# Rotary sums of q and k: accumulating DMAs in place of GpSimd additions

## The chip, the cores and the metric

The kernel runs on one core of a Trainium2 chip. A core has five engines that follow instruction streams of their own: TensorE (PE: matmuls and transposes), VectorE (DVE), ScalarE (ACT), GpSimd (POOL) and SyncE (SP, which issues DMAs), and 16 DMA engines that move data. The metric is the device time of one execution in microseconds (us), lower is better. The kernel before takes 3546.09 us, the median of three runs (3543.17 to 3550.35).

## The reference

The input x has 8 sequences of 512 tokens with 128 features, in float32. It is normalised, and two branches are added to it: an attention with relative positions (16 heads of 8), and a stack of six layers, each a local attention (16 heads of 64, windows of 32) and a gated feed-forward part. The change lies in the local attention, where q and k are normalised per head and rotated:

```python
def attn_layer(x, Wqkv, qs, ksc, Wo):
    qkv = x @ Wqkv
    q, k, v = jnp.split(qkv, 3, -1)
    ...
    q = l2norm(q) * qs
    k = l2norm(k) * ksc
    ...
    q = q * cos * scale + rotate_half(q) * sin * scale
    k = k * cos * inv + rotate_half(k) * sin * inv
    out = local_attention(q, k, v)
    ...
    return out @ Wo
```

## The kernel before

There are two stages. The relative attention (`rel_attention`) takes up about the first 470 us. The layers (`steps_of_layers`) follow: 6 layers x 8 sequences x 4 blocks of 128 tokens are 192 tiles, numbered by `tiles`. Weights are reloaded for each layer. x stays transposed in SBUF (`xt`).

The tiles run in a software pipeline. The loop at L1113 takes a tile n, and a word from `ORDERS` (line 48) sets the order of steps within it: `p0` to `p3` project tile n+2, `r` normalises it, `q0 q1 k0 k1` transpose q and k of tile n+1 on TensorE (`turn`, L818), `s0 s1` are the scores and the softmax of tile n, `v0` to `v3` its values, `a0 a1` apply the softmax of tile n-1, `+` adds tile n-2 into `xt`, and `f` is one step of a feed-forward. There are four such words, one for each tile of a sequence. TensorE keeps the order in which the program is written (`manual_schedule`). The order on the other engines is chosen when the program is built, by a timeline that the scheduler keeps, so a change of one step can move others.

For a tile, `project(n, c)` runs four times: c = 0, 1 for the two halves of q, c = 2, 3 for those of k. TensorE makes a half (128 tokens x 512) in PSUM out of three matmuls (L637 to L639). VectorE multiplies it twice, by the cosine table into `q` (L762) and by the sine table into `rot` (L763), with the halves of each head exchanged, and ScalarE squares it into `sq` (L764). When the second half is there, GpSimd adds `rot` to `q`, 128 x 1024 (L767). For q GpSimd also adds the two halves of `sq` (L769), and VectorE sums them per head into `ss` (L770); for k VectorE sums both halves itself (L772). `normalise` (step `r`) works out the inverse roots `rn` on VectorE (L782, and L70 to L81 in `rsqrt`), and GpSimd scales first q and then k by them (L786). The buffers are rings: 4 of `q`, 3 of `rot`, 2 of `sq`, so a buffer of `rot` is written again three sums later.

Beside this, GpSimd scales the softmax (`pr`, L888, which waits for the sums `sm` inverted at L887), and makes some low parts (L626) and diagonal matrices (`dg`, L985) for the feed-forward. Values are copied out of PSUM by ScalarE (`v`, L904, 3 buffers) and laid out anew by 16 DMAs of 64 KB per tile from SyncE's queue (`vw`, L906); TensorE reads them at L924. ScalarE's exponentials (L871) wait for the row maxima `mx` of VectorE (L858).

Of the kernel before, what the change touches and what calls it, by code (L numbers as in the profile page):

```python
# [16 lines left out]
ALU = mybir.AluOpType  # L17
# [572 lines left out]
def steps_of_layers(ctx, tc, i, ident, ident_b, xt, out, spare):  # L590
    nc = tc.nc
# [41 lines left out]
    def product(ps, lhs, rhs):  # L633


        (ah, al), (bh, bl) = lhs, rhs
        nc.tensor.matmul(ps, lhsT=ah, rhs=bh, start=True, stop=False)  # L637
        nc.tensor.matmul(ps, lhsT=ah, rhs=bl, start=False, stop=False)  # L638
        nc.tensor.matmul(ps, lhsT=al, rhs=bh, start=False, stop=True)  # L639
# [96 lines left out]
    def halves(xs, t):  # L736
        return [x[:, t * P : (t + 1) * P] for x in xs]

    def project(n, c):

        part, a = divmod(c, 2)
        l, b, t = tiles[n]
        if c == 0:
            ready[n] = {"ss": pq.tile([P, 2, H], F32, name="ss")}
        if a == 0:
            ready[n][part] = [
                pq.tile([P, H, 2, D // 2], F32, name="q", bufs=4),
                pq.tile([P, H, 2, D // 2], F32, name="rot", bufs=3),
                pq.tile([P, 2, H, D // 2], F32, name="sq"),
            ]  # L750
        q, v, sq = ready[n][part]
        xs, w, ss = streams[l, b], projections[l, part], ready[n]["ss"]
        cos, sin = (
            tables[l, t][:, 2 * part + m, :].rearrange("p (a d) -> p a d", a=2) for m in range(2)
        )

        def wide(x):
            return x.unsqueeze(1).to_broadcast([P, H, D // 2])

        ps = ps_qk.tile([P, H, D // 2], F32, name="qk_ps")  # L760
        product(ps.rearrange("p h d -> p (h d)"), halves(xs, t), w[a])
        nc.vector.tensor_mul(q[:, :, a], ps, wide(cos[:, a, :]))  # L762
        nc.vector.tensor_mul(v[:, :, 1 - a], ps, wide(sin[:, 1 - a, :]))  # L763
        nc.scalar.activation(sq[:, a], ps, AF.Square)  # L764
        if a == 0:
            return
        nc.gpsimd.tensor_add(q, q, v)  # L767
        if str(part) in VAR["C"]:
            nc.gpsimd.tensor_add(sq[:, 0], sq[:, 0], sq[:, 1])  # L769
            nc.vector.tensor_reduce(ss[:, part, :], sq[:, 0], AX.X, ALU.add)  # L770
        else:
            nc.vector.tensor_reduce(  # L772
                ss[:, part, :], sq.rearrange("p a h d -> p h a d"), AX.XY, ALU.add
            )
        ready[n][part] = q.rearrange("p h a d -> p h (a d)")
# [311 lines left out]
    for n in range(2):  # L1087
        for c in range(4):
            project(n, c)
            if c == 3:  # L1090
                normalise(n)
            yield
# [19 lines left out]
    with tc.manual_schedule(engines={nc.tensor.engine}):  # L1112
        for n in range(-1, len(tiles) + 2):  # L1113
# [10 lines left out]
            for step in ORDERS[n % NT].split():  # L1124
                kind, k = step[0], int(step[1:] or 0)
                if kind == "p" and more:
                    project(n + 2, k)
                    l, b, t = tiles[n + 2]
                    if k == 3 and b == B - 1 and l + 1 < DEPTH:
# [123 lines left out]
```

## Time and profile before

| | us |
|---|---|
| median of three runs | 3546.09 |
| profiled execution, its own time | 3550.94 |
| its span, first to last instruction | 3549.2 |
| GpSimd: 384 additions q + rot (L767), 2400 ns each | 921.7 |
| GpSimd: 384 scalings (L786), 1909 ns each | 725.1 |
| GpSimd: 192 scalings of the softmax (L888), 1906 ns each | 366.0 |
| VectorE: 768 products into q (L762), 682 ns each | 523.7 |
| VectorE: 768 products into rot (L763), 680 ns each | 522.0 |
| ScalarE: 768 squares (L764), 649 ns each | 490.4 |
| SyncE: issue of one vw DMA (L906), 3072 of them, median | 0.583 |

The profile is that of one execution. "Busy" is the time in which an engine executes; issuing a DMA is not counted as busy. A row such as `x384 | 921.7, 2400 | 114.8 <-DVE rot L763 96.5` says: 384 instructions, 921.7 us busy in all, 2400 ns each, and 114.8 us in which the engine was idle just before one of them, of which 96.5 us ended when VectorE's `rot` at L763 was ready. The chain follows the end of the run back through what released each step. The mean granted TensorE clock is 0.982 of full speed. The DMA engines are busy 28.8% of the span with the queue of SyncE and ScalarE; no DMA is issued by GpSimd.

### The profile page before, as it was taken

To read this page: it belongs to the slowest core of one execution; us is meant where nothing else is said; L and a number is where in the kernel's file an instruction comes from. 1 tells how busy PE (TensorE), PEld (TensorE's weight loads), DVE (VectorE), ACT (ScalarE), POOL (GpSimd) and SP (SyncE) were. 2 spreads that over 40 slices of the span, in tenths; PEclk is the share of its full clock that TensorE was granted. 3 is DMA by queue.
4 is the path that set the end of the run, shared out by engine and by line. 5 is a ranking of instruction groups with operands and counts; after the bars stand their busy time and mean duration, and the time that the engine had idled before them with its cause. 6 is when DMAs were issued, how large, how long until landed. Compare 5 with 4: busy or idle time off the path is not lost.

```text
span 3549.2 us, 130709 instructions
## 1 busy us (share of the span) xinstructions
PE 3354.5 (95%) x49936; PEld 2523.3 (71%) x49936; DVE 3054.2 (86%) x7155; ACT 2899.2 (82%) x10268; POOL 2955.1 (83%) x2274
## 2 busy tenths in 40 slices
PE   6999988999999999899999999999999999999997
PEld 4666656777777777677777677776777776777775
DVE  8788757988899898889988888989989899888884
ACT  3777657888888888798988789897888988888885
POOL 5666657998888999898999889998888988989894
PEclk9999989999999999999999999999999999999998
DMA  1111123323333333333333333333323233333332
GB/s 42 35 29 41 29 63 71 73 70 74 76 89 73 72 75 71 89 76 74 71 76 76 90 72 70 75 71 84 87 68 76 69 76 88 74 79 74 84 77 58
DMA packets 221060, 249.93 MB, mean 70 GB/s; under 512 B 73238, under 2 KB 115604, under 8 KB 220436
## 3 DMA queue, kind: packets, MB, share of 16 engines
q1 hardware_dynamic: 220148, 241.18, 28.8%
q8 instruction: 397, 6.50, 0.8%
q14 instruction: 227, 1.86, 0.2%
q10 hardware_dynamic: 288, 0.39, 0.0%
HBM read 26.92 MB, written 4.19 MB: 9 GB/s over the span
## 4 chain that ended last, share of the span: by engine, by line
PE 32%; ACT 19%; POOL 14%; DVE 12%; issue 3%; DMA 2%; SPq 1%; ACTq 0%; POOLq 0%; DVEq 0%
ACT pr L871 6%; POOL q L786 5%; PE qkT_ps L818 5%; PE sc_ps L850 4%; PE y_ps L924 4%; POOL pr L888 3%; PE v_ps L637 3%; ACT sq L764 2%; PE qk_ps L637 2%; POOL q L767 2%; PE v_ps L638 2%; PE f_ps L1040 2%; PE v_ps L639 2%; ACT h L1015 2%; DVE ss L772 2%
## 5 line engine op out<-in xcount | busy, mean ns | idle before, releaser
L767 POOL TENSOR_TENSOR q<-q,rot 128x1024 f32<-128x1024 f32 x384 | 921.7, 2400 | 114.8 <-DVE rot L763 96.5
L871 ACT ACTIVATE pr<-sc_ps,mx 128x64 f32<-128x64 f32 x3072 | 928.9, 358 | 95.7 <-DVE mx L858 95.0
L871 ACT ACTIVATION_READ_ACCUMULATOR pr<-sc_ps,mx 128x1 f32 x3072 | 746.1, 250 | 0.0
L786 POOL TENSOR_TENSOR q<-q,rn 128x1024 f32<-128x1024 f32 x384 | 725.1, 1909 | 10.3 <-DVE rn L81 10.3
L764 ACT ACTIVATE sq<-qk_ps 128x512 f32<-128x512 f32 x768 | 490.4, 649 | 197.7 <-DVE rot L763 196.6
L762 DVE TENSOR_TENSOR q<-qk_ps,wrot 128x512 f32<-128x512 f32 x768 | 523.7, 682 | 37.4 <-PE qk_ps L639 28.4
L763 DVE TENSOR_TENSOR rot<-qk_ps,wrot 128x512 f32<-128x512 f32 x768 | 522.0, 680 | 0.0
L904 ACT COPY v<-v_ps 128x512 f32<-128x512 f32 x768 | 477.9, 676 | 48.5 <-DMA vw<-v 29.0
L888 POOL TENSOR_TENSOR pr<-pr,sm 128x1024 f32<-128x1024 f32 x192 | 366.0, 1906 | 164.8 <-DVE sm L887 92.5
L818 PE MATMUL qkT_ps<-ident,q 128*128 128x128 f32 x3072 | 477.6, 282 | 8.0 <-POOL q L786 4.2
L850 PEld LDWEIGHTS sc_ps<-kT,qT 64*32 64x32 f32 x24576 | 363.8, 108 | 129.1 <-issue 126.9
L818 PEld LDWEIGHTS qkT_ps<-ident,q 128*128 128x128 f32 x3072 | 346.9, 142 | 114.2 <-issue 27.1
L850 PE MATMUL sc_ps<-kT,qT 64*32 64x64 f32 x24576 | 426.4, 219 | 1.5 <-ACT kT L822 1.5
L924 PE MATMUL y_ps<-vw,pT 128*32 128x128 f32 x11904 | 386.5, 276 | 4.1 <-DMA vw<-v 2.6
L924 PEld LDWEIGHTS y_ps<-vw,pT 128*32 128x32 f32 x11904 | 331.9, 110 | 59.3 <-issue 40.8
L637 PE MATMUL qk_ps<-wqk_hi,xs_hi 128*128 128x512 f32 x768 | 339.6, 442 | 32.8 <-ACT sq L764 32.2
L637 PE MATMUL v_ps<-wvo_hi,xs_hi 128*128 128x512 f32 x768 | 339.7, 442 | 24.4 <-DVE xt L945 13.2
L639 PE MATMUL qk_ps<-wqk_hi,xs_lo 128*128 128x512 f32 x768 | 307.5, 400 | 0.0
L638 PE MATMUL qk_ps<-wqk_lo,xs_hi 128*128 128x512 f32 x768 | 306.9, 400 | 0.0
L822 ACT COPY kT<-qkT_ps 128x512 f32<-128x512 f32 (+1 forms) x672 | 304.9, 536 | 0.2 <-PE qkT_ps L818 0.2
L639 PE MATMUL v_ps<-wvo_hi,xs_lo 128*128 128x512 f32 x768 | 304.1, 396 | 0.0
L638 PE MATMUL v_ps<-wvo_lo,xs_hi 128*128 128x512 f32 x768 | 302.5, 394 | 0.0
(207 smaller groups left out, 7615.3 us busy)
## 6 DMA issues: line engine op xcount, KB each, us to landing
vw<-v SPq DMA_DIRECT2D x3072, 64.0 KB
a_qz<-a_qT SPq DMA_DIRECT2D x128, 64.0 KB
wqk_raw<-in_Wqk SPq DMA_DIRECT2D x24, 256.0 KB
wv_raw<-in_WvT SPq DMA_DIRECT2D x12, 256.0 KB
wo_raw<-in_Wo SPq DMA_DIRECT2D x12, 256.0 KB
wrot<-in_trig SPq DMA_DIRECT2D x24, 128.0 KB
a_x<-in_x SPq DMA_DIRECT2D x8, 256.0 KB
a_res<-in_x SPq DMA_DIRECT2D x8, 256.0 KB
```

The lines of the kernel that those rows point to most:

```text
L637: nc.tensor.matmul(ps, lhsT=ah, rhs=bh, start=True, stop=False)
L638: nc.tensor.matmul(ps, lhsT=ah, rhs=bl, start=False, stop=False)
L639: nc.tensor.matmul(ps, lhsT=al, rhs=bh, start=False, stop=True)
L762: nc.vector.tensor_mul(q[:, :, a], ps, wide(cos[:, a, :]))
L763: nc.vector.tensor_mul(v[:, :, 1 - a], ps, wide(sin[:, 1 - a, :]))
L764: nc.scalar.activation(sq[:, a], ps, AF.Square)
L767: nc.gpsimd.tensor_add(q, q, v)
L786: nc.gpsimd.tensor_mul(q, q, r[:, m, :].unsqueeze(2).to_broadcast([P, H, D]))
L818: nc.tensor.transpose(tr[:, m, :], q[:, 2 * hp : 2 * hp + 2, :].rearrange("p h d -> p (h d)"), ident)
L850: nc.tensor.matmul(ps[32 * j : 32 * j + 32, g, w, :], lhsT=qT[r, 4 * g + j, W * w : W * w + W], rhs=kT[r, 4 * g + j, W * w : W * w + 2 * W ...
L871: nc.scalar.activation(pr[:, p, g, w, :], ps[:, g, w, :], AF.Exp, bias=mx[:, p, g, w : w + 1], **kw,),
L924: nc.tensor.matmul(y[W * w : W * w + W, :], lhsT=pT[:, p, g, w, half, :], rhs=v[:, p, g, :], start=(p, g, half) == (0, 0, 0 if keys[w] is ...
```

## The change

In `project`, the addition of `rot` (named `v` there) to `q` is no longer a tensor_tensor of GpSimd. GpSimd issues a DMA instead, from SBUF to SBUF, which reads `rot` and adds it to what stands in `q`. It is issued from GpSimd's queue, once for q and once for k of each tile, 512 KB each (128 partitions x 4 KB). Everything that reads `q` afterwards (L786) waits for the landing of that DMA, and so does the next writer of the buffer of `rot` (L763). The addition of the squares at L769 stays on GpSimd.

```diff
         nc.scalar.activation(sq[:, a], ps, AF.Square)
         if a == 0:
             return
-        nc.gpsimd.tensor_add(q, q, v)
+        nc.gpsimd.dma_start(out=q, in_=v, accum_op=ALU.add)
         if str(part) in VAR["C"]:
             nc.gpsimd.tensor_add(sq[:, 0], sq[:, 0], sq[:, 1])
             nc.vector.tensor_reduce(ss[:, part, :], sq[:, 0], AX.X, ALU.add)
```

## The prediction

> **What bounds the kernel now.** I read the page's busy rows, then the chain of work that ended last, then sums over the stretch of the six layers, then GpSimd's own timeline and the waits.
>
> The page of the kernel before: busy rows, chain, and the rows of the two GpSimd steps at issue.
>
> ```profile
> PE 3354.5 (95%) x49936; PEld 2523.3 (71%) x49936; DVE 3054.2 (86%) x7155; ACT 2899.2 (82%) x10268; POOL 2955.1 (83%) x2274
> ...
> q1 hardware_dynamic: 220148, 241.18, 28.8%
> ...
> PE 32%; ACT 19%; POOL 14%; DVE 12%; issue 3%; DMA 2%; SPq 1%; ACTq 0%; POOLq 0%; DVEq 0%
> ACT pr L871 6%; POOL q L786 5%; PE qkT_ps L818 5%; PE sc_ps L850 4%; PE y_ps L924 4%; POOL pr L888 3%; PE v_ps L637 3%; ACT sq L764 2%; PE qk_ps L637 2%; POOL q L767 2%; PE v_ps L638 2%; PE f_ps L1040 2%; PE v_ps L639 2%; ACT h L1015 2%; DVE ss L772 2%
> ...
> L767 POOL TENSOR_TENSOR q<-q,rot 128x1024 f32<-128x1024 f32 x384 | 921.7, 2400 | 114.8 <-DVE rot L763 96.5
> ...
> L786 POOL TENSOR_TENSOR q<-q,rn 128x1024 f32<-128x1024 f32 x384 | 725.1, 1909 | 10.3 <-DVE rn L81 10.3
> ```
>
> TensorE is busy 95% and yet only 32% of the chain: the end passes from engine to engine. L767 is 921.7 us of GpSimd's work, but 2% of the chain.
>
> Sums over the stretch in which L767 runs (columns: stretch, its length, busy us and count per engine, TensorE clock, DMA share, GB/s):
>
> ```profile
> 470.00:3480.00 3010.00, 2878.01 (x46426) 2214.30 (x46426) 2664.76 (x6046) 2568.69 (x9501) 2646.43 (x1521) 0.99 0.32 76
> ```
>
> 192 tiles in 3010 us are 15.7 us a tile. TensorE idles 132 us here: whatever GpSimd is relieved of, no more than that 4% can come back. GpSimd works 13.8 us of each 15.7, of which two adds are 4.8.
>
> GpSimd's timeline over one tile (start, us, instruction, idle before it):
>
> ```profile
> 1537.39 2.41 POOL L767 TENSOR_TENSOR q<-q,rot 128x1024 f32<-128x1024 f32 x1
> 1539.76 1.27 POOL L769 TENSOR_TENSOR sq<-sq 128x512 f32<-128x512 f32 x1
> 1542.20 2.40 POOL L767 TENSOR_TENSOR q<-q,rot 128x1024 f32<-128x1024 f32 x1 [1.17 <-DVE rot L763]
> 1544.55 1.10 POOL L626 TENSOR_TENSOR fx_lo<-xt,fx_hi 128x512 fp32r<-128x512 f32 x1
> 1547.14 1.91 POOL L888 TENSOR_TENSOR pr<-pr,sm 128x1024 f32<-128x1024 f32 x1 [1.49 <-DVE sm L887]
> 1549.00 3.77 POOL L786 TENSOR_TENSOR q<-q,rn 128x1024 f32<-128x1024 f32 x2
> 1552.73 2.40 POOL L767 TENSOR_TENSOR q<-q,rot 128x1024 f32<-128x1024 f32 x1
> ```
>
> Two things stand here. GpSimd has idle time after the second add, before L888 (or, in other tiles, L985 or L786), and what ends it is VectorE. So the adds are not what makes L888 and L786 late. And the scaling of k (the second half of L786) begins at 1550.9, 8.7 us after the add of k: that is the room a slower sum has.
>
> The waits, longest first (engine, line, what it waited for: us, times, longest):
>
> ```profile
> ACT pr L871 <- DVE mx L858: 95.0, 91, 3.5
> ...
> DVE ss L770 <- POOL sq L769: 34.8, 73, 1.3
> ...
> ACT v L904 <- DMA vw<-v: 29.0, 23, 2.6
> ...
> PEld qkT_ps L818 <- POOL q L786: 24.0, 42, 1.2
> ```
>
> **Removed.** 384 adds of 2.400 us on GpSimd. What of this was on the path: 2% of 3549.2 us is 71 us, or 71/2.4 = 30 adds.
>
> **Added, the issue.** 384 DMA issues on GpSimd. No row shows one. The nearest is SyncE's issue of a vw DMA, median 583 ns (32 rows); that is the low bound, and the add's own 2.4 us the high one, above which nothing is relieved. A software issue of 128 rows lies above SyncE's: I take 1.2 us. GpSimd then gets 2 x (2.4 - 1.2) = 2.4 us a tile. On the path it is 30 x 1.2 = 36 us at most, and since the idle above shows VectorE arriving last at the next step, I keep half: **-18 us** (0 to -36).
>
> A rule speaks against the issue. The Trainium skill (SBUF — State Buffer, SBUF: two separate sides) says that GpSimd can't write the descriptors of its DMAs while VectorE runs an operation in a 2-port mode, as an fp32 copy within SBUF is. The row: VectorE's commonest work here (L762, L763, L858) reads PSUM. Its long SBUF-only operation is the transpose L890, 1.23 us, once a tile. If each met one of the two issues the cost would be 192 x 1.23 = 236 us of GpSimd time, inside the 461 us relieved; the row says it is rare, so I take 0 and leave it to the range.
>
> **Added, the transfer.** Each moves 512 KB, 32.8 KB per DMA engine. By the queue row, 28.8% of 16 x 3549.2 us moved 241.18 MB: 14.7 KB per us and engine, so 2.2 us if the sum costs one pass and 4.5 us if two reads take turns. The Trainium skill (Collectives: The Full Stack, The bandwidth ceiling: the fold count and why AG ≠ RS ≠ AR) says that a reducing transfer runs at half the rate of a copy, since it reads two sources, and gives about 31 GB/s per engine: an estimate of 32.8/15.5 = 2.1 us by its rate, 4.5 us by its factor on the row. The row decides for the rate, the rule warns of the factor: 2.2 to 4.5. Shared with the 0.32 that the engines already carry, 3.2 to 6.6. Fixed: a 64 KB vw DMA in the chain takes 1.95 us to land, of which 4 KB per engine is 0.3, so 1.7. From the start of the issue: 1.2 + 1.7 + 3.2 to 6.6 = **6.1 to 9.5 us**, middle 7.8.
>
> The room, from GpSimd's timeline between 1490 and 1700 us: from the start of k's add to k's scaling 7.3 us in the shortest of 13 tiles, mostly 8.2 to 9.6. For q it is 9.4 or more. Behind that TensorE takes k's transposes (L818) 2.1 us or more after the scaling ended. So middle and most of the span are hidden. What covers it is the chain ss, rn on VectorE, and L888 on GpSimd. One tile in four scales before L888 (with hl of L626 in front), so there a late k delays pr: 48 tiles, up to 9.5 - 8.4 = 1.1 us each, 53 us at the far end, nothing at the middle: **+10 us**. Behind a waiting L786 stand L888 or the next tile's issue and sq add.
>
> **Buffers.** rot (3 buffers) comes free at the landing, not the add's end. Its next writer, L763, comes three sums later, some 18 us at two per 15.7 us: no cost below that latency.
>
> **Contention.** 384 x 512 KB take 2 x (2.2 to 4.5) us of each 15.7 on all DMA engines: share 0.32 becomes 0.60 to 0.89. A vw DMA has two 2 KB rows per engine, each may find one 4 KB row in front (0.28 to 0.56 us): about 0.84 us when it meets one, 0.43 of the time, so 0.36 us. The chain's DMA part is 2%, 71 us, about 30 landings at 2 to 3 us: +11. ACT's wait for v's buffers, 29.0 us now, by a quarter: +7. **+18 us**.
>
> **Moved on VectorE.** The program order of the changed kernel has L770 (sum of sq) ahead of one more instruction than before in most tiles. In 41 tiles it now stands ahead of the maximum L858, which TensorE's scores and then ACT's exponentials wait on: 41 x 0.60 us = 25 us at most. ACT waits for mx in 91 of 384 cases, some more when it is later: half, **+12 us**. In exchange L770's own wait of 34.8 us in all mostly goes, if the issue is shorter than the add. TensorE's order is the same.
>
> **Sum** for the profiled execution: 3550.9 (span 3549.2) - 18 + 10 + 18 + 12 = 3573. It lies 4.9 us above the median of the runs, so about **3568 us** there.
>
> **The rivals.**
> *Faster.* All of the 36 us is kept, transfers land in one pass, and vw isn't disturbed: 3546 - 36 = 3510; with part of the costs 3525 to 3535. For it: L770 waits for POOL, TensorE for L786 24 us, and GpSimd is at 88% in the layers. Against: the idle before L888, and TensorE's 132 us as a ceiling.
> *The landing bounds GpSimd's loop.* One mechanism: GpSimd is in order, so from k's issue to the next k's issue it must fit landing, k's scaling 1.9, the next q issue 1.2 and sq add 1.3. That is over 15.6 when a landing takes over 11.2 us. At 4.5 us of transfer and little left of the engines, k queues behind q: q lands 9.5 after its issue, k 6.6 later, at 16.1, which is 12 us after its own issue (4.1 later). 0.8 us x 192 = 154 us: **3700**; at 13 us 3890. For it: nothing here shows what an accumulate costs. Against: the row's rate.
> *No change.* Relief and costs cancel: 3546.
> *It relieves nothing.* If an issue holds GpSimd 2.4 us, the -18 is gone: 3586, within my forecast's range.
>
> **How the numbers follow.** Forecast, slightly slower, 3554 to 3610: 0.36. Landing bounds: 0.20. Faster: 0.28. No change: 0.16. About 0.2%, 7 us, is what a measurement of this kernel can tell from no change. So faster 0.28, same 0.16, slower 0.56. Range 3515 to 3750: under it the full relief with nothing paid (0.05), over it landings beyond 12.3 us (0.12).
>
> **What would show it.** GpSimd's busy time in the layers falls by 922 us; the gap around each issue gives 1.2 us right or wrong. The wait L786 <- DMA should be small; if it is hundreds of us, the second rival holds. DMA share 0.60 to 0.89. ACT v <- DMA should rise over 29 us. If TensorE's idle falls well below 132 us, I was wrong on the sign.

## The result and the profile after

| | us | ratio to before, 95% interval |
|---|---|---|
| before, measured beside the change | 3544.63 | |
| after | 3606.23 | 1.0163 [1.0145, 1.0181] |
| forecast | 3568 | 1.006 |

The change costs 61.6 us where 22 were forecast (3568 less 3546). The profiled execution has a span of 3604.5 us at a granted TensorE clock of 0.983, against 0.982 before, and the mean over the runs is 0.985 against 0.981, so a lower clock is not the cause of the loss.

The page after: busy rows, the two DMA queues (packets, MB, share of 16 engines), the chain by engine and by line, two groups of instructions, and the row of the new DMA.

```profile
PE 3368.5 (93%) x49936; PEld 2533.3 (70%) x49936; DVE 2999.9 (83%) x7155; ACT 2911.0 (81%) x10268; POOL 2360.3 (65%) x2274
...
q0 software_dynamic: 55296, 201.35, 30.9%
...
q1 hardware_dynamic: 220148, 241.18, 27.1%
...
PE 42%; ACT 22%; DMA 11%; DVE 11%; SPq 6%; POOL 4%; issue 3%; ACTq 0%; POOLq 0%; DVEq 0%
DMA vw<-v 9%; ACT pr L871 7%; SPq L906 6%; PE y_ps L924 5%; PE qkT_ps L818 5%; PE sc_ps L850 4%; ACT sq L764 3%; PE v_ps L637 3%; PE qk_ps L637 2%; PE v_ps L638 2%; PE v_ps L639 2%; ACT h L1015 2%; PE f_ps L1040 2%; PE a_o_ps L467 2%; ACT v L904 2%
...
L904 ACT COPY v<-v_ps 128x512 f32<-128x512 f32 x768 | 474.8, 643 | 140.9 <-DMA vw<-v 97.7
...
L767 POOL DMA_DIRECT2D q<-rot x384 | 332.2, 865 | 367.2 <-DVE xt L945 115.4
...
q<-rot POOLq DMA_DIRECT2D x384, 512.0 KB, 5.8
```

GpSimd did get free: its busy time fell by 595 us (the 332 us of its own issues are counted as busy here), and its share of the chain from 14% to 4%. But DMA and SyncE's queue went from 3% of the chain to 17%, nearly all of it `vw`. (The chain of before breaks off 589 us after the start, so its shares add up to 83% and not to 100%; `vw` alone went from 54 to 315 us.) The new transfer is not on the chain at all. It lands 5.8 us after the start of its issue, well before anyone needs it. It is seen in another way: the queue q0 takes 30.9% of the DMA engines' time, more than all the other transfers take.

The waits after (engine, line, what it waited for: us in all, times, longest):

```profile
PEld qk_ps L637 <- ACT sq L764: 126.0, 115, 4.7
...
ACT v L904 <- DMA vw<-v: 97.7, 84, 6.5
...
PE qk_ps L637 <- ACT sq L764: 80.6, 67, 4.5
...
ACT pr L871 <- DVE mx L858: 56.6, 73, 3.7
...
PE y_ps L924 <- DMA vw<-v: 32.3, 47, 2.3
...
DVE ss L770 <- POOL sq L769: 10.6, 10, 1.9
```

The rows of TensorE's wait for the squares in the kernel before:

```profile
PEld qk_ps L637 <- ACT sq L764: 72.0, 109, 3.7
...
PE qk_ps L637 <- ACT sq L764: 32.2, 29, 3.2
```

Before, ACT waited 29.0 us for buffers of `v`, now 97.7. ACT then comes late to its squares, and TensorE waits for those (L637). No L786 <- DMA wait appears in the list: no scaling waits for a landing. And L871's wait for the row maxima is smaller than before (95.0), not larger.

Two stretches of the chain after, in order of time (start, us, what):

```profile
1565.60 0.59 SPq L906
...
1566.23 3.58 DMA vw<-v
...
1616.06 0.59 SPq L906
...
1616.69 5.99 DMA vw<-v
```

The same two of the 3072 transfers (the 12th of the 66th tile, the 16th of the 69th), from the start of the issue to the landing, took 1.98 and 1.97 us before. From all vw transfers of a trace, each from the start of its issue to its last landing:

| landing of a vw transfer, us | mean | median | 75% | 90% |
|---|---|---|---|---|
| before | 2.24 | 1.98 | 2.22 | 3.09 |
| after | 3.18 | 2.76 | 4.20 | 5.13 |

Row by row, vw isn't slower: a 2 KB row of it took 148 ns (median) before and 124 ns after. It comes later, because rows of the new transfer, 339 ns each for 4 KB, stand in front of it on the same DMA engines: 128 rows on 16 engines are 8 for each, 2.7 us.

### The profile page after: what moved, and what is told of

The parts are those of the page before. It is cut to its first block, busy times and chain, and to the rows that moved or that the text cites. A ratio compares the mean times of both kernels' runs of the same rounds, so it can differ in the third digit from the quotient of the medians.

```text
span 3604.5 us, 131258 instructions
## 1 busy us (share of the span) xinstructions
PE 3368.5 (93%) x49936; PEld 2533.3 (70%) x49936; DVE 2999.9 (83%) x7155; ACT 2911.0 (81%) x10268; POOL 2360.3 (65%) x2274
## 3 DMA queue, kind: packets, MB, share of 16 engines
q0 software_dynamic: 55296, 201.35, 30.9%
q14 instruction: 230, 1.88, 0.2%
## 4 chain that ended last, share of the span: by engine, by line
PE 42%; ACT 22%; DMA 11%; DVE 11%; SPq 6%; POOL 4%; issue 3%; ACTq 0%; POOLq 0%; DVEq 0%
DMA vw<-v 9%; ACT pr L871 7%; SPq L906 6%; PE y_ps L924 5%; PE qkT_ps L818 5%; PE sc_ps L850 4%; ACT sq L764 3%; PE v_ps L637 3%; PE qk_ps L637 2%; PE v_ps L638 2%; PE v_ps L639 2%; ACT h L1015 2%; PE f_ps L1040 2%; PE a_o_ps L467 2%; ACT v L904 2%
## 5 line engine op out<-in xcount | busy, mean ns | idle before, releaser
L871 ACT ACTIVATE pr<-sc_ps,mx 128x64 f32<-128x64 f32 x3072 | 925.8, 355 | 58.1 <-DVE mx L858 56.6
L786 POOL TENSOR_TENSOR q<-q,rn 128x1024 f32<-128x1024 f32 x384 | 722.9, 1901 | 33.7 <-DVE rn L81 33.6
L871 ACT ACTIVATION_READ_ACCUMULATOR pr<-sc_ps,mx 128x1 f32 x3072 | 742.0, 248 | 0.0
L764 ACT ACTIVATE sq<-qk_ps 128x512 f32<-128x512 f32 x768 | 481.6, 637 | 172.0 <-DVE rot L763 164.7
L904 ACT COPY v<-v_ps 128x512 f32<-128x512 f32 x768 | 474.8, 643 | 140.9 <-DMA vw<-v 97.7
L762 DVE TENSOR_TENSOR q<-qk_ps,wrot 128x512 f32<-128x512 f32 x768 | 523.3, 681 | 78.5 <-PE qk_ps L639 69.1
L767 POOL DMA_DIRECT2D q<-rot x384 | 332.2, 865 | 367.2 <-DVE xt L945 115.4
L763 DVE TENSOR_TENSOR rot<-qk_ps,wrot 128x512 f32<-128x512 f32 x768 | 521.4, 679 | 0.0
L924 PE MATMUL y_ps<-vw,pT 128*32 128x128 f32 x11904 | 415.5, 278 | 34.4 <-DMA vw<-v 32.3
L924 PEld LDWEIGHTS y_ps<-vw,pT 128*32 128x32 f32 x11904 | 342.3, 111 | 108.7 <-issue 65.0
L637 PE MATMUL qk_ps<-wqk_hi,xs_hi 128*128 128x512 f32 x768 | 337.5, 439 | 81.1 <-ACT sq L764 80.6
L637 PE MATMUL v_ps<-wvo_hi,xs_hi 128*128 128x512 f32 x768 | 339.8, 442 | 15.9 <-ACT qT L822 9.6
L772 DVE TENSOR_REDUCE ss<-sq 128x16 f32<-128x1024 f32 x192 | 233.4, 1216 | 103.9 <-ACT sq L764 100.8
```

Of the source, the lines that this page charges most:

```text
L786: nc.gpsimd.tensor_mul(q, q, r[:, m, :].unsqueeze(2).to_broadcast([P, H, D]))
L871: nc.scalar.activation(pr[:, p, g, w, :], ps[:, g, w, :], AF.Exp, bias=mx[:, p, g, w : w + 1], **kw,),
L904: ecopy(VAR['v'][j])(v, ps)
L924: nc.tensor.matmul(y[W * w : W * w + W, :], lhsT=pT[:, p, g, w, half, :], rhs=v[:, p, g, :], start=(p, g, half) == (0, 0, 0 if keys[w] is ...
```

## The experiments

Theory **T** (traffic): the loss is the time the DMA engines spend on the sums, which delays `vw`; the relief of GpSimd is real and larger than forecast. Rivals: **W**, that somebody waits for the landing; **S**, that the scheduler's other order on VectorE and ScalarE costs the time; **A**, that accumulating in itself disturbs something. All results first; each ratio is against runs of the kernel before made beside that version (medians 3544.6 to 3553.0), so ratios are compared below, not medians. "vw" is the 90% point of the landing, "ACT v" the wait of ACT for buffers of `v`, "fx_lo" the mean duration of one operation of VectorE that becomes important below.

| kernel | median us | ratio, 95% interval | q0 share | vw, us | ACT v, us | fx_lo, ns |
|---|---|---|---|---|---|---|
| before | | 1 | none | 3.09 | 29.0 | 1050 |
| after | 3606.23 | 1.0163 [1.0145, 1.0181] | 30.9% | 5.13 | 97.7 | 816 |
| e_relief | 3490.93 | 0.9848 [0.9822, 0.9874] | none | 3.19 | 27.3 | 742 |
| e_traffic | 3602.26 | 1.0157 [1.0133, 1.018] | 30.9% | 5.19 | 103.0 | 822 |
| e_copy | 3483.73 | 0.9829 [0.9802, 0.9856] | 15.6% | 3.89 | 24.5 | 777 |
| e_copy2 | 3592.67 | 1.011 [1.0072, 1.0147] | 30.4% | 5.12 | 94.2 | 908 |
| e_half | 3491.45 | 0.9818 [0.9792, 0.9844] | 17.7% | 3.72 | 29.6 | 820 |
| e_split | 3589.68 | 1.0106 [1.0085, 1.0127] | 34.2% | 4.77 | 91.1 | 1445 |
| e_qonly | 3537.46 | 0.9972 [0.9961, 0.9983] | 15.8% | 4.63 | 17.8 | 1333 |
| e_konly | 3540.66 | 0.997 [0.996, 0.9981] | 15.6% | 3.80 | 60.6 | 1110 |
| e_v4 | 3569.07 | 1.0049 [1.0033, 1.0065] | 31.3% | 5.19 | 5.6 | 814 |
| b_v4 | 3538.43 | 0.9957 [0.9932, 0.9982] | none | 3.17 | 3.9 | 1006 |
| q_v4 | 3525.42 | 0.993 [0.9912, 0.9949] | 15.8% | 4.62 | 1.7 | 1226 |
| r_q | 3556.49 | 1.001 [0.9999, 1.002] | none | 3.25 | 26.7 | 2299 |
| r_k | 3508.55 | 0.9892 [0.9872, 0.9912] | none | 3.08 | 27.8 | 1135 |
| h_half | 3616.86 | 1.02 [1.0178, 1.0222] | 16.9% | 3.62 | 28.0 | 3552 |
| h_half_v4 | 3604.3 | 1.0163 [1.0146, 1.0179] | 16.9% | 3.63 | 2.3 | 3560 |
| h_half_g | 3565.78 | 1.0038 [1.0025, 1.0051] | 17.1% | 3.65 | 22.9 | off VectorE |
| b_g | 3575.64 | 1.007 [1.0053, 1.0087] | none | 3.14 | 21.3 | off VectorE |
| q_v4_g | 3548.52 | 0.9994 [0.9984, 1.0003] | 15.8% | 4.68 | 2.2 | off VectorE |

### Relief and traffic apart

A cut of code that takes out the DMA is against the changed kernel, one that takes out the addition against the kernel before.

**e_relief**: neither addition nor transfer.

```diff
-        nc.gpsimd.dma_start(out=q, in_=v, accum_op=ALU.add)
```

> The sum of q and rot is left out altogether (neither an addition on GpSimd nor a DMA), so q and k keep their cosine part alone. Theory A (the DMA engines are shared: vw lands later because of the new traffic): without the traffic the time falls to the kernel before or a little under it, 3520 to 3546 us, and ACT v <- DMA vw is back near 29 us. Theory B (the scalings L786 and the next writer of rot wait for the landing): also 3520 to 3546 us. Theory C (VectorE's changed order, or the order of any engine): the time stays near 3600 us, since the order is that of a short GpSimd step.

**e_traffic**: the transfer as after, but `rot` is accumulated onto itself, so that no reader of `q` waits for it.

```diff
-        nc.gpsimd.dma_start(out=q, in_=v, accum_op=ALU.add)
+        nc.gpsimd.dma_start(out=v, in_=v, accum_op=ALU.add)
```

> The accumulating DMA adds rot to rot itself instead of to q: same bytes, same issue on GpSimd, but no reader waits for it (only the next writer of rot). q and k keep their cosine part alone. Theory A: the whole loss stays, 3595 to 3615 us, and ACT v <- DMA vw stays near 98 us. Theory B: the time falls to that of the kernel with the sum left out, 3520 to 3546 us.

**e_copy**: a plain copy of the same bytes to the same place, with the same waits.

```diff
-        nc.gpsimd.dma_start(out=q, in_=v, accum_op=ALU.add)
+        nc.gpsimd.dma_start(out=q, in_=v)
```

> The DMA copies rot over q without adding (one read instead of two), so q and k keep their sine part alone; issues, waits and destination are those of the changed kernel. Theory A with the engines' time as the cause: a 4 KB row takes some 170 ns instead of 339, the new queue's share falls from 30.9% to some 15%, and half to three quarters of the loss goes, 3555 to 3580 us. If the number of transfers or the wait counts and not their length: 3595 to 3610 us.

With neither, the time falls 1.5%, 54 us, under every range that was expected: the relief is larger than any of the theories had it. The copy too came out far under both of its ranges. With the traffic that nobody waits for it is where the change is: **W falls**. With the copy it is as low as with no transfer: the waits for `q` are all there, and the order of instructions of e_traffic and of e_copy is that of the changed kernel on every engine, so **S falls** as the cause of the loss. What differs between e_copy and after is the queue's row and what it does to `vw`. From e_copy:

```profile
q0 software_dynamic: 55296, 201.35, 15.6%
...
q<-rot POOLq DMA_DIRECT2D x384, 512.0 KB, 4.1
```

```profile
ACT v L904 <- DMA vw<-v: 24.5, 28, 2.0
```

```profile
PE 53%; ACT 19%; DVE 13%; POOL 6%; DMA 4%; issue 3%; SPq 2%; ACTq 0%; POOLq 0%; DVEq 0%
ACT pr L871 7%; PE qkT_ps L818 6%; PE sc_ps L850 6%; PE y_ps L924 5%; PE v_ps L637 4%; PE qk_ps L637 3%; PE v_ps L638 3%; PE v_ps L639 3%; DMA vw<-v 3%; PE qk_ps L639 3%; PE qk_ps L638 3%; PE f_ps L1040 2%; ACT sq L764 2%; POOL q L786 2%; PE a_o_ps L467 2%
```

The same 201.35 MB in the same 55296 packets take half the DMA engines' time: a 4 KB row 162 ns as a copy, 339 ns as a sum. ACT's wait for buffers is no more than it was before the change. The loss is 1.0163 - 0.9829 = 3.3%, 118 us.

### Engine time, or accumulating itself

**e_copy2**: the copy, and a second one of the same size to HBM. It takes the same engine time as a sum, with no accumulation. (The line that declares the scratch tensor isn't shown.)

```diff
-        nc.gpsimd.dma_start(out=q, in_=v, accum_op=ALU.add)
+        nc.gpsimd.dma_start(out=q, in_=v)
+        nc.gpsimd.dma_start(out=i["scratch"][2 * n + part], in_=v.rearrange("p h a d -> p (h a d)"))
```

> Two plain copies in place of each accumulate: rot over q, and rot to a scratch region in HBM that nothing reads; so q and k keep their sine part alone. The bytes read and the engines' time are near those of the accumulate (two rows of some 160 to 200 ns for one of 339), but no row adds. Theory A2 (the engines' time that stands in front of vw decides): vw lands as late as in the changed kernel, ACT v <- DMA vw 80 us or more, 3590 to 3620 us. Theory A1 (the length of the single accumulating row decides): near the single copy, 3480 to 3520 us, ACT v <- DMA vw under 45 us.

**e_half**: the sum, but for half the heads; it takes the engine time of a copy, with accumulation.

```diff
-        nc.gpsimd.dma_start(out=q, in_=v, accum_op=ALU.add)
+        nc.gpsimd.dma_start(out=q[:, : H // 2], in_=v[:, : H // 2], accum_op=ALU.add)
```

> Heads 0 to 7 alone get their sine part added: 256 KB per DMA instead of 512 KB, in rows of 2 KB, as many issues as in the changed kernel. Theory A2: half the engines' time, so a loss as with q alone or k alone (some 45 to 60 us over the kernel with the sum left out), 3520 to 3550 us. If the number of transfers counts: 3580 us or more.

**e_split**: the whole sum in two transfers with 2 KB rows, to see whether it is the long row that blocks.

```diff
-        nc.gpsimd.dma_start(out=q, in_=v, accum_op=ALU.add)
+        for h in (slice(0, H // 2), slice(H // 2, H)):
+            nc.gpsimd.dma_start(out=q[:, h], in_=v[:, h], accum_op=ALU.add)
```

> Each accumulating DMA is cut in two, heads 0 to 7 and 8 to 15: the same bytes in rows of 2 KB, twice as many issues on GpSimd. Theory A1 (a vw row waits behind the one accumulating row that an engine is at, and the length of that row counts): rows half as long, ACT v <- DMA vw falls from 98 to 50 to 70 us and the time to 3560 to 3590 us. Theory A2 (what counts is how much of the engines' time the accumulates take, and how much of it stands queued in front of vw): no change, 3590 to 3620 us.

From e_copy2, the queue and the wait, and then the queue of e_half:

```profile
q0 software_dynamic: 110592, 402.70, 30.4%
```

```profile
ACT v L905 <- DMA vw<-v: 94.2, 87, 3.4
```

```profile
q0 software_dynamic: 55296, 100.69, 17.7%
```

Two copies lose nearly as the sum does, at the same share and with the same landing of `vw` (VectorE's order differs here, and GpSimd has a second issue); half a sum, with VectorE's order unchanged, loses nothing. So **A falls** as the main cause, and the engine time of the sums decides; the 0.5% between two copies and a sum stays open. Shorter rows barely help (1.0106; that kernel's VectorE order differs from after's, so the 0.6% between them isn't put down to the rows).

What the versions with a loss share is the time that one call of the step puts on each DMA engine at a stretch. Worked out from the rows (8 for each engine and transfer), it is 2.7 us for a sum, 2.6 for two copies (160 ns a row) and 2.9 for a sum in two halves (179 ns a row of 2 KB); it is 1.3 us for a copy and 1.5 for half a sum (188 ns), which lose nothing. The share of q0 in the whole span is not the measure, as e_konly shows below.

### Where the delay enters

**e_v4**: the changed kernel with a fourth buffer for `v`, and one for `ys` to make room; **b_v4**: the same in the kernel before, the control.

```diff
-        v = p3.tile([P, 512], F32, name="v")
+        v = p3.tile([P, 512], F32, name="v", bufs=4)
...
-        ys = p2.tile([P, E], F32, name="ys")
+        ys = p2.tile([P, E], F32, name="ys", bufs=1)
```

> The changed kernel with 4 buffers of v instead of 3 (and 1 of ys instead of 2, to make room). If the loss comes in through ACT's copy that waits for a v buffer still being read by vw's DMA, that wait goes under 30 us and the time falls by 40 to 70 us, 3535 to 3565 us. If it comes in through TensorE's y_ps, which waits for the landed vw, no buffer helps: 3590 to 3610 us.

> The kernel before with 4 buffers of v (and 1 of ys): a control for the two runs with 4 buffers. ACT v <- DMA vw is 29 us there, so 3530 to 3550 us; what it falls by is not to be counted as a cure of the DMA's cost.

From e_v4:

```profile
PE y_ps L924 <- DMA vw<-v: 52.8, 62, 1.9
...
PEld y_ps L924 <- DMA vw<-v: 41.9, 50, 2.2
...
ACT v L904 <- DMA vw<-v: 5.6, 11, 1.0
```

The fourth buffer takes 92 us of ACT's waits away and 1.1% of the time, of which the control gets 0.4% too. TensorE's own waits for `vw` grow from 60 to 95 us. So ACT's ring of three is one entry of the delay and L924 another; 1.0049 is still 2% above the 0.985 without traffic.

### One sum by DMA

**e_qonly** sends only q's sum by DMA, **e_konly** only k's. **q_v4** is e_qonly with the four and one buffers of above.

```diff
-        nc.gpsimd.dma_start(out=q, in_=v, accum_op=ALU.add)
+        if part == 0:
+            nc.gpsimd.dma_start(out=q, in_=v, accum_op=ALU.add)
+        else:
+            nc.gpsimd.tensor_add(q, q, v)
```

(`part == 1` for e_konly.)

> Only the sum of q goes by the accumulating DMA, that of k is GpSimd's addition again: half the new traffic. Theory A: some half of the 62 us, 3565 to 3590 us, ACT v <- DMA vw 50 to 70 us. Theory B (the landing of k is the late one, with q's room 9.4 us and more): the loss goes, 3535 to 3550 us.

> Only the sum of k goes by the accumulating DMA, that of q is GpSimd's addition. If half the traffic costs the same wherever it falls, the time is that of the kernel with q alone, 3530 to 3545 us. If k's transfer is the one that falls on the burst of vw (v0 to v3), 3560 to 3590 us and ACT v <- DMA vw above 50 us.

> The sum of q alone by DMA, and 4 buffers of v. If the buffers of v let in most of the loss, this keeps the relief of the q addition and pays less: 3505 to 3530 us. If not, as with 3 buffers: 3530 to 3545 us.

**r_q** and **r_k** are these without any transfer: the kernel before, with the sum of q, or of k, left out.

```diff
-        nc.gpsimd.tensor_add(q, q, v)
+        if part == 1:
+            nc.gpsimd.tensor_add(q, q, v)
```

(`part == 0` for r_k.)

> The sum is left out for q and kept as GpSimd's addition for k: half of the relief without any DMA. If relief is worth the same for each addition, 3515 to 3525 us (half of the 56 us); then the DMA of q costs the rest up to 3537 us, some 15 us, far under half of the 113 us that both cost. If the first half of the relief brings most, 3490 to 3505 us, and the DMA of q costs some 40 us.

> The kernel before with the sum left out for k only (so k lacks its rotated product); q keeps its GpSimd add, and no DMA is issued. Theory (VectorE is held while a GpSimd add runs on the same buffers' side, and k's add is the one that falls on fx_lo): fx_lo goes from 1050 ns before, and from 2299 ns with q's sum left out, to about 740 to 1000 ns, and the time to 3490 to 3520 us. Rival (the relief is GpSimd's queue, and half of it gives half): about 3520 us with fx_lo near 1050 ns. If neither sum alone gives anything, about 3545 us: then the relief needs both gone.

The clean pair is e_konly and r_k, which have the same order on VectorE and ScalarE: e_konly (0.997) lies 0.8% above r_k (0.9892), so k's traffic alone costs some 28 us, at a share of 15.6% that was free when each transfer was half as long. For q there is no such pair: e_qonly (0.9972) lies under r_q (1.001), but their VectorE orders differ and r_q loses time elsewhere, as follows. The range of theory A for e_qonly, and both ranges for r_q, missed; theory B's range for e_qonly was met, though its reason, a late landing of k, had fallen with W. q_v4 is the fastest complete version of this study, 0.993.

Each sum delays other transfers. Mean landing of the 16 `vw` transfers of a tile, four for each of `v0` to `v3`, from the traces:

| landing, us | v0 | v1 | v2 | v3 |
|---|---|---|---|---|
| before | 2.22 | 2.30 | 2.21 | 2.19 |
| e_qonly | 3.65 | 2.54 | 2.23 | 2.69 |
| e_konly | 2.23 | 3.33 | 2.32 | 2.25 |
| after | 3.99 | 3.52 | 2.38 | 2.75 |

By the 90% point of all landings q's sum does more harm (4.63 us, against 3.80 for k's), yet ACT waits for buffers 17.8 us with q's and 60.6 with k's; q's shows at L924 instead, where TensorE's waits for `vw` are 40 us, against 8 before and with k's. So the 90% point of the landings doesn't tell the cost by itself; it matters which transfer is late, and who needs it.

The relief doesn't add up either: 1.5% with both sums gone, 1.1% for k's alone, nothing for q's alone. In r_q one VectorE operation stands out, `fx_lo` of the feed-forward (xs + bias - fx_hi, both tensors in SBUF), 48 times. The group in before and in r_q:

```profile
L1004 DVE SCALAR_TENSOR_TENSOR fx_lo<-fx,wg,fx_hi 128x512 fp32r<-128x512 f32 x48 | 50.4, 1050 | 2.8 <-ACT fx_hi L1003 2.8
```

```profile
L1005 DVE SCALAR_TENSOR_TENSOR fx_lo<-fx,wg,fx_hi 128x512 fp32r<-128x512 f32 x48 | 110.4, 2299 | 2.0 <-ACT fx_hi L1004 2.0
```

and in r_q's timeline:

```profile
1566.69 2.38 POOL L768 TENSOR_TENSOR q<-q,rot 128x1024 f32<-128x1024 f32 x1 [0.91 <-PE sc_ps L851]
...
1567.06 2.56 DVE L1005 SCALAR_TENSOR_TENSOR fx_lo<-fx,wg,fx_hi 128x512 fp32r<-128x512 f32 x1
```

It starts while GpSimd adds and ends 0.55 us after it; alone it takes 0.74 us. The expectation for r_k, that fx_lo would fall to 740 to 1000 ns, missed (1135), while its time was within what was expected. So the 1.1% of r_k came without any relief of fx_lo, at an order of VectorE that differs from before's in only 52 of 7155 places; what is left for it is GpSimd's own queue, and 27 us less of VectorE's time in other subtractions, of weights (`wqk_lo`, `w_lo`). In r_q fx_lo took 60 us more than in before, and the order differs in 889 places; that the held fx_lo is what cancels q's relief is likely, but not shown.

### Half the heads, and the held operation

**h_half** completes e_half: a DMA for heads 0 to 7, an addition on GpSimd for heads 8 to 15. **h_half_v4** has four buffers for `v` and one for `ys`.

```diff
-        nc.gpsimd.dma_start(out=q, in_=v, accum_op=ALU.add)
+        nc.gpsimd.dma_start(out=q[:, : H // 2], in_=v[:, : H // 2], accum_op=ALU.add)
+        nc.gpsimd.tensor_add(q[:, H // 2 :], q[:, H // 2 :], v[:, H // 2 :])
```

> A complete version: heads 0 to 7 of q and k are summed by an accumulating DMA of 256 KB, heads 8 to 15 by a GpSimd add of 128x512. Theory (the loss is the DMA engines' time ahead of vw, and half of it is free): the half traffic costs nothing, as where the other half was left out (0.982), and the two half adds give back about 2.4 us of GpSimd work in each tile: 3500 to 3530 us, with ACT's waits for vw's buffers near 30 us in sum. Rival (half the traffic is only free when GpSimd has nothing to add): 3545 us or more.

> The kernel with half its heads summed by DMA, and four buffers for v and one for ys. Theory: the remaining waits for vw's buffers go (30 us to under 5 in sum), and the control of these buffers in the kernel before gave 0.4%: 3485 to 3515 us, below every complete version so far. Rival (the waits turn up at y_ps, as they did with the whole traffic): no better than the same kernel with three buffers.

Both missed: 1.02 and 1.0163, neither better than the change itself. The traffic isn't why: `vw` lands as in e_half (3.62 us) and ACT waits 28.0 us. The relief is smaller than expected: GpSimd's busy time fell by 115 us from before (2955.1 to 2840.6), where 2.4 us a tile would be 461. What stands out is on VectorE, by the group and the timeline of h_half:

```profile
L1005 DVE SCALAR_TENSOR_TENSOR fx_lo<-fx,wg,fx_hi 128x512 fp32r<-128x512 f32 x48 | 170.5, 3552 | 1.7 <-ACT fx_hi L1004 1.7
```

```profile
617.54 1.54 POOL L768 TENSOR_TENSOR q<-q,rot 128x512 f32<-128x512 f32 x1
...
618.77 1.54 POOL L770 TENSOR_TENSOR sq<-sq 128x512 f32<-128x512 f32 x1
618.92 4.09 DVE L1005 SCALAR_TENSOR_TENSOR fx_lo<-fx,wg,fx_hi 128x512 fp32r<-128x512 f32 x1
...
619.99 1.15 POOL L767 DMA_DIRECT2D q<-rot  x1
...
620.60 1.86 POOL L768 TENSOR_TENSOR q<-q,rot 128x512 f32<-128x512 f32 x1
```

fx_lo begins when an addition of GpSimd (L770) has just begun, and lasts through it, the DMA issue and the next addition; it ends 0.55 us after that, as in r_q. Over 48 such operations that is 48 x (3552 - 742) = 135 us of VectorE held, 120 more than in before; behind it stand the row maxima, and ACT's wait for them is 167.0 us here (95.0 before). VectorE's order differs from before's in only 64 places, so the order is a weak rival for the 2% that h_half loses against before. Against e_half it stands 3.8% higher, 135 us of 3546 (the expectation below has 125, from medians), and there 514 places differ. How much of this is fx_lo was tried by taking it off VectorE: ScalarE adds the bias in place, and GpSimd subtracts. **h_half_g** is h_half so, **q_v4_g** the fastest version, **b_g** the control in the kernel before.

```diff
-        nc.scalar.activation(hi, xs, AF.Identity, bias=bias)
-        nc.vector.scalar_tensor_tensor(lo, xs, bias, hi.bitcast(F32), ALU.add, ALU.subtract)
+        nc.scalar.activation(xs, xs, AF.Identity, bias=bias)
+        split(hi, lo, xs, nc.gpsimd)
```

> The kernel with half its heads summed by DMA, and fx_lo taken off VectorE: ScalarE adds the bias to xs in place, and GpSimd subtracts (48 operations of about 1.3 us there, about 0.6 us more on ScalarE). GpSimd can't hold up an operation that stands in its own queue. Theory (half the DMA traffic is free, and the 125 us that this kernel stands above the one with the other half left out are fx_lo's: 3552 ns instead of 742 each, 135 us of VectorE in sum): the time falls to 3480 to 3530 us, and VectorE's busy time by some 170 us. Rival (it is GpSimd's own queue, 625 us of half adds): it stays above 3600 us, and rises with the 62 us more on GpSimd.

> The best complete version so far (only q by DMA, four buffers for v, one for ys: 0.993 of before), with fx_lo taken off VectorE in the same way. Theory: of the 58.8 us that fx_lo takes there all leaves VectorE, 23 us of it time in which it was held: 3490 to 3520 us. Rival (GpSimd, which still adds k, has no room for 62 us more): 3525 us or more.

> The control: the kernel before with fx_lo on GpSimd and nothing else. Theory: 50 us leave VectorE, 15 of them held time, and 62 us come to GpSimd, the busier of its queues: 3520 to 3550 us. If it gains as much as the half version does, the held time was not what that one lost.

None fell where the theory put it, and h_half_g lies between theory and rival. It gains 1.6% on h_half, 57 us, though GpSimd has 85 us of subtractions more to do, and ACT's wait for the maxima goes from 167.0 to 90.4 us. The same move alone, in b_g, costs 0.7%, 25 us. So an estimate for the held VectorE is 57 us, or some 82 if the move costs in h_half what it costs in b_g; the rest of the 135 us is GpSimd's own time or the order, and is open. In q_v4, where fx_lo was held for 23 us in all, the move loses more than it gains.

The order of VectorE's instructions is the same in after, e_traffic, e_copy, e_half and e_v4, and in r_k and e_konly. It differs in hundreds of the 7155 places between before and after (504), e_relief (871) or r_q (889), and in 52 and 64 between before and r_k or h_half. Differences of half a per cent between versions of unlike order could be that; no run separates it.

## Why the prediction was wrong in size

Two terms of the sum were far too small, and they cancelled in the forecast (-18 and +18). The +22 us that were left came from the two terms that came to nothing (below). So the sign came right by luck, though the mechanism behind it, a shared DMA engine that delays `vw`, was named.

**The contention term failed (+18 us forecast).** It measures 112 us (1.0163 - 0.9848, of 3546) against e_relief, 118 against e_copy. The step that failed is "each may find one 4 KB row in front": it made +0.36 us for a mean transfer, and was given to some 30 landings of the chain and to a quarter more of ACT's waits. Measured, the mean landing rose by 0.94 us and the 90% point by 2.0. Two rows of 339 ns in front make 0.68 us, and SyncE's issue of a `vw`, which is within the landing, got longer by 0.8 at its own 90% point; together that is short of 2.0, so by this estimate more than one row of the sum stands in front of a row of `vw`. The price was then put on the chain and the waits of before. But ACT's waits for buffers tripled where a quarter was forecast, and `vw` came to 9% of the chain and SyncE's queue to 6%: transfers that were early enough before became late enough to be on the chain. It isn't proportional: in e_copy the mean landing rose from 2.24 to 2.67 us, more than the forecast's 0.36, at no cost.

**The relief term failed (-18 us, at most -36).** It measures -54 us without any issue (e_relief), -61 with 384 issues of a copy (e_copy) and -65 with 384 issues of 865 ns (e_half). What failed are the two cuts that the forecast made in the 71 us of L767 on the chain. The first took off half for an issue of 1.2 us in place of an add of 2.4. But the three versions that free 2.4, 1.8 and 1.5 us for each add gain about the same, within their intervals: the issue cost nothing that shows. The second kept half of the rest, since VectorE arrives last at GpSimd's next step. But most of the chain's share did come back, so that idle time was no proof that the adds make nothing late. The 71 us themselves (85 before rounding, 2.4% of the span, from a chain that covers 83% of it) were not exceeded. In e_copy POOL's share of the chain fell from 14% to 6%, 8 points where L767's own were 2: the scalings that stand behind the adds went with them (L786 from 5% to 2%).

A second part was not in the forecast at all: the adds hold VectorE's operations with two SBUF inputs. The section of the Trainium skill that was weighed for the descriptors (SBUF — State Buffer, SBUF: two separate sides) says so: such an operation and a GpSimd one that reads SBUF take a pair of ports in turns, for a whole instruction. The forecast read it for the added issue, and not for the additions that go. VectorE's busy time falls by 59 us from before (3054.2) to e_relief (2994.9) with the same work, 44 us of it in three subtractions of two SBUF inputs (`wqk_lo`, `fx_lo`, `w_lo`). How the 54 us divide between GpSimd's queue, this holding and the other order of VectorE was not settled; k's 1.1% in r_k came with fx_lo as long as before. The granted clock is a further rival: its mean over the runs is 0.981 in before, 0.987 in e_relief and 0.989 in e_copy. Among the 94 recorded runs of before, the time falls by about 2.4 us for each 0.001 of clock, so by this estimate 14 us of e_relief's 54 and 19 of e_copy's 61 go along with the clock; whether it is a cause or follows from the relief is open. TensorE's 132 us did hold as a ceiling.

**What was right.** The range, and the part that DMA engines play. The issue of 1.2 us was 0.865, between the two ends given (but a copy's took 0.582, no more than SyncE's, so 128 rows alone don't make an issue longer). The transfer, 5.8 us from the start of its issue, lay just under the 6.1 to 9.5 computed. The rule from the Trainium skill (Collectives: The Full Stack, The bandwidth ceiling) that a reducing transfer runs at half a copy's rate holds here: 339 against 162 ns for a row. The DMA share in the layers, forecast at 0.60 to 0.89, is 0.66, and TensorE's idle time in that stretch rose from 132 to 177 us:

```profile
470.00:3480.00 3010.00, 2832.91 (x45491) 2181.37 (x45493) 2563.76 (x5926) 2527.04 (x9310) 2011.41 (x1487) 0.99 0.66 140
```

The descriptor rule (SBUF — State Buffer, SBUF: two separate sides), taken at 0, shows little: GpSimd's issues last 820 to 1201 ns, with a median of 867, so none stands more than 0.4 us above the shortest.

**Terms that came to nothing.** A late k (+10 us): no L786 waits for a DMA, so the rival in which the landing bounds GpSimd's loop is false as well; it needed 11.2 us, and the longest landing took 8.2. The moved L770 (+12 us): ACT waits less for the maxima than before, 56.6 us. The wait of L770 for `sq` went from 34.8 to 10.6 us, as written.

The measured -54 and +112 add up to +58 us, near the 61.6 of the change, but that is no test of them: both are differences to e_relief.

## What to carry to other kernels

Before work is moved to DMA, price it in DMA engine time (a sum costs two copies here), and ask how long one transfer occupies each engine at a stretch and which small, urgent transfers with few buffers come just behind it. Here 1.3 to 1.5 us at a stretch were free and 2.6 to 2.9 for q and k were not; k's sum alone, at half the share, still cost 0.8%, and for q's alone no run tells. A mean of the landings says little, and even a late one costs only where somebody needs it. The chain's share of a line gave a fair ceiling here for what its removal brings; a shorter step in its place brought as much. And an addition on GpSimd can cost VectorE time, so read the durations of VectorE's SBUF-only operations beside GpSimd's timeline before and after a move.

## What was not expected of the hardware

- A VectorE operation with two SBUF inputs, 0.74 us alone, took 2.56 us beside an addition of GpSimd and 4.09 us beside two of them with a DMA issue between: by the rule it waits for the instruction that holds the ports, but here it also stayed behind the next one (GpSimd had no idle time between them). GpSimd's operations grew less: the half addition's median is 1.57 us, its longest 1.88 us. Operations of VectorE on PSUM beside it kept their length (L762, from PSUM and SBUF, has a median of 682 ns in before and 683 in h_half, and 694 at the longest in both).
- An accumulating DMA within SBUF takes 339 ns for a 4 KB row, and a copy 162; its 512 KB land 5.8 us after the start of the issue, a copy's 4.1. GpSimd spends 865 ns on the issue, and 582 on a copy's.
- SyncE's own issues of `vw` get longer under the load: the 90% point goes from 0.60 to 1.38 us.
